# A masked attention layer in 2x2 block products: two PSUM copies taken with a pair's opening products, two weight differences put behind the first sums, adjacency searches put later, the last rows scattered by halves

## The chip, the core and the metric

The kernel runs on one core of one Trainium2 chip. The metric is the device time of one execution in microseconds. Five engines work from queues of their own, each in order: PE (matmul; its weight loads are listed as PEld), DVE (VectorE), ACT (ScalarE), POOL (GpSimd) and SP, which here only issues transfers. POOL issues the indirect transfers (gathers and scatters by row number), ACT a few stores.

## The reference

A graph attention layer over 2708 rows of 1024 float32 features. The adjacency matrix has about four ones in a row.

```
h = relu(layernorm(x))
q, k, v = h @ W_q.T + b_q, h @ W_k.T + b_k, h @ W_v.T + b_v
z = (q @ k.T) / sqrt(1024) * adj;   z = where(z == 0, -10000, z)
out = x + relu(softmax(z, axis=1) @ v)
```

## The kernel before

**Algebra.** `q @ k.T` is `h @ M @ h.T` with `M = W_q.T @ W_k`, computed first (`part_of_m`, L353, 256 recorded matmuls). One neighbour's score is then a dot product of a row of `h @ M` with the neighbour's row of `h`. The weighted sum of the neighbours' rows of h is formed first and multiplied by `W_v` afterwards. Rows are sorted by their number of neighbours, so that a tile of 128 rows takes K gathers.

**Pairs.** The 2708 rows are 21 full tiles and a rest. Two large products (h by M, and weighted sums by `W_v`) are made for pairs of tiles, 10 pairs each, numbered n = 0 to 9 (q pairs) and 10 to 19 (o pairs); tile 0 comes before the q pairs and one sorted tile (`alone`, tile 11) after the o pairs. A pair is a 2x2 block matrix (two tiles by two halves of the features), multiplied by a 2x2 block weight with seven block products in place of eight. The left operands are the blocks `a11`, `a12`, `a22` and the sums `s1` to `s4`; the right operands are the blocks M[i, j] and four differences T[0..3] (`ts_of_m`, L422; one is a [128 x 2048] subtraction on DVE). One block product is four matmuls of 128x512 in the code (`add_block`, L779); the profile records eight for them, since each float32 matmul is recorded twice.

**The order in one pair** (`multiply`, L793). X, Z and Y are PSUM banks of a pool of four. The opening products of the next pair are issued inside the current pair (`opened`, L784): `X += a11 M11` and `Z += s1 T0`. Then, for the pair itself: Y is a copy of X (L799), p5 a copy of Z (L802), both on ACT; `Y += s2 T1`; u2 a copy of Y (L806); `X += a12 M21`, result c11; `Z += s4 M22`, result c12 = Z + u2 (DVE, L844); `Y += s3 T2`, result c22 = Y + p5 (DVE, L841); then the next pair's opening products; `Y += a22 T3`, result c21. So on PE c22 stands between the s3 product and the a22 product of the same bank Y.

**Other work during the pairs.** A function `after(i)` is called between these steps. It transposes the rows of pair n + 1 on PE (`half_turned`, L274), forms s1 to s4 (L529), seeds the banks (L554), and loads the rows of pair n + 2: natural rows (tiles `h_e`, on SP, L562) for n + 2 < FIRST = 5, sorted rows (`qr`, gathered by POOL, L435) from there on. In the first pairs it also runs the rest of the layer norm and of the adjacency reading, from the table `steps_at` (L580): `s16-17` loads x tiles and takes their statistics, `r` takes the root, `a` applies the norm on ACT (L233) and stores h to `h_dram` on POOL, and `eN` (`edges`, L255) loads adjacency tile N (1354 KB, SP, three buffers in turn), sums its rows on ACT (`sized`, L261) and finds its columns with four index searches on DVE (L264) and six small operations.

**The sort.** After all tiles are searched `sort` (L472, called at pair 2, step 3) counts with two matmuls (L493, L495), computes the place of each row (`pos_i`, L507), scatters the table of neighbours to DRAM by place (`put`, L450: 11 indirect stores for the second part, the sorted tiles 11 to 21) and loads it back (`tab`, L461); then come the first gathers of `qr` rows, and the same for the first part.

**Who sets the order.** ACT's order is the program's up to the sort. DVE's order is the program's from pair FIRST on; before that, and for the other engines throughout, a scheduler that works on estimates places the instructions when the kernel is built. All queues are then fixed. From pair FIRST on, a stream of scores and weighted sums (`attention`, L730) is spread over DVE, with gathers on POOL.

**The end.** The lone tile's weighted sum goes through four block products; its result is added to its rows of x (`y_alone`) and written by one indirect store, `scatter` (L616).

Of the kernel before, what the change touches and what calls it, by code (L numbers as in the profile page):

```python
# [10 lines left out]
FT = mybir.dt.float32  # L11
U32 = mybir.dt.uint32
# [3 lines left out]
ALU = mybir.AluOpType  # L16
AX = mybir.AxisListType

P = 128
NB = 512  # L20
# [3 lines left out]
SLOTS = 16  # L24
# [31 lines left out]
def tile_preln_masked_attention(  # L56
# [12 lines left out]
    nc = tc.nc  # L69
    N, D = x.shape  # L70
    DC = D // P
    NH = D // NB
# [17 lines left out]
    psum = ctx.enter_context(tc.tile_pool(name="psum", bufs=4, space=bass.MemoryType.PSUM))  # L90
# [34 lines left out]
    ptab = tab  # L125
# [50 lines left out]
    stat = ph.enter_context(tc.tile_pool(name="stat", bufs=4, side="right"))  # L176
# [242 lines left out]
    def small(name):  # L419
        return half.tile([P, NB], FT, tag="half", name=name, bufs=14)  # L420

    def ts_of_m(*which):  # L422
        flat = M.rearrange("p i j c w -> p i j (c w)")
        t = T.rearrange("p k c w -> p k (c w)")
        for k in which:
            a, b = ((flat[:, 0, 1], flat[:, 0, 0]), (flat[:, 1, 1], t[:, 0]), (flat[:, 1, 1], flat[:, 0, 1]),
                    (flat[:, 1, 0], t[:, 1]))[k]
            nc.vector.tensor_sub(t[:, k], a, b)
# [8 lines left out]
    rows_of = {}  # L437
    FIRST = (EARLY - SINGLE) // 2
# [77 lines left out]
    behind = []  # L516
# [44 lines left out]
            if t > 1:  # L561
                nc.sync.dma_start(row, h_dram[t * P:(t + 1) * P, :])  # L562

    ts_of_m(0, 1, 2, 3)

    nc.vector.tensor_sub(bp_sb[:, NB:], bp_sb[:, NB:], bp_sb[:, :NB])
    natural_rows(0)
# [9 lines left out]
    q = query(hT.pop(0), banks, "e0", first=True, between=('e11 a s16-17', ''), mid=open_first)  # L577
    nc.scalar.dma_start(q_dram[0:P, :], q)

    steps_at = {(0, 0): 'e12 r a e13', (0, 3): 'e14 s18-19 r e15', (1, 0): 'a e16 s20-21 e17', (1, 3): 'e18 r a e19', (2, 0): 'e20 e21'}  # L580
    
    slots, free = [], []

# [16 lines left out]
    def ts_of_wv():  # L600
        with tc.issue_after(placed[0].ins):
            for c in range(4):
                b11, b12 = slots[2 * c][:, :NB], slots[2 * c][:, NB:]
                b22, b21 = slots[2 * c + 1][:, :NB], slots[2 * c + 1][:, NB:]
                nc.vector.tensor_sub(b11, b12, b11)
                nc.vector.tensor_sub(b12, b22, b12)
                nc.vector.tensor_sub(b22, b22, b11)
                nc.vector.tensor_sub(b21, b21, b22)
                for k, r in enumerate((b11, b22, b12, b21)):
                    nc.sync.dma_start(tv_dram[k][:, c, :], r)  # L610
# [5 lines left out]
    outs = []  # L616

    def scatter(y, t, n):
        to = nc.gpsimd.indirect_dma_start(  # L619
            out=out, out_offset=bass.IndirectOffsetOnAxis(ap=ptab.bitcast(U32)[:n, t, SLOTS:SLOTS + 1], axis=0),  # L620
            in_=y[:n], in_offset=None)
        for other in outs:
            tc.declare_no_dep(to.ins, other.ins, reason="rows of a permutation")
        outs.append(to)
# [154 lines left out]
    def add_block(bank, a, b, last=True):  # L779
        for c in range(4):  # L780
            mm = nc.tensor.matmul(bank, a[:, c, :], b[:, c, :], start=False, stop=(c == 3), skip_group_check=True)  # L781
        return mm

    def opened(n):  # L784

        if n not in banks_of:
            return
        X, Z = banks_of[n]
        ops = ops_of[n][0]
        add_block(X, ops["a11"], M[:, 0, 0])  # L790
        products.append(add_block(Z, ops["s1"], T[:, 0]))

    def multiply(n, results, after):  # L793


        X, Z = banks_of.pop(n)
        ops = ops_of.pop(n)[0]
        Y = psum.tile([P, NB], FT, tag="acc", name="psy")
        nc.scalar.copy(Y, X)  # L799
        after(0)  # L800
        p5 = small("p5")
        nc.scalar.copy(p5, Z)  # L802
        after(1)
        products.append(add_block(Y, ops["s2"], T[:, 1]))
        u2 = small("u2")
        nc.scalar.copy(u2, Y)  # L806
        after(2)
        add_block(X, ops["a12"], M[:, 1, 0])
        results[0](X)
        after(3)  # L810
        add_block(Z, ops["s4"], M[:, 1, 1])
        results[2](Z, u2)
        after(4)
        products.append(add_block(Y, ops["s3"], T[:, 2]))
        results[1](Y, p5)
        after(5)
        if n != FIRST - 1:
            opened(n + 1)
        add_block(Y, ops["a22"], T[:, 3])
        results[3](Y)  # L820
        if n == FIRST - 1:

            opened(n + 1)
        after(6)

    lo, hi = slice(0, NB), slice(NB, D)
# [77 lines left out]
    def of_wv(i, j):  # L904

        return wv[j][:, i * 4:(i + 1) * 4, :]
# [4 lines left out]
    alone = order[-1]  # L911
    units = [("q",) + p for p in q_pairs] + [("o",) + p for p in o_pairs]
# [29 lines left out]
    for n, unit in enumerate(units):  # L942
        kind, ta, tb = unit
        now[0] = n
        if n == FIRST:
            ordered.enter_context(tc.manual_schedule(engines={mybir.EngineType.DVE}))
        if FIRST - 1 <= n <= FIRST + 2:

            i, j = ((0, 0), (0, 1), (1, 0), (1, 1))[n - FIRST + 1]
            nc.sync.dma_start(m_dram[i, j], M[:, i, j])  # L950
        share = (20.0 if kind == "q" else 19.0) / 7
        nxt = units[n + 1] if n + 1 < len(units) else None
        results = (q_results if kind == "q" else o_results)(ta, tb)

        def after(i):
            if (n, i) == (2, 3):
                with tc.issue_after(products[-1].ins):
                    placed.append(sort())
                ordered.close()
                ts_of_wv()  # L960
            if n == FIRST - 1 and i == 5:

                chain.append(behind[-1])
                next(stream)
            if n == FIRST - 1 and i == 6:
                chain.append(behind[-1])
            if (n, i) >= (FIRST, 0):
                advance(share)
            if nxt is not None:

                if i == (3 if n == FIRST - 1 else 0):
                    ops_of[n + 1] = blocks(*rows_of[n + 1], nc.gpsimd if n + 1 < FIRST - 1 else None)
                    ops_of[n + 1][1]()
                if i == (4 if n == FIRST - 1 else 2):
                    ops_of[n + 1][2]()
                    rows_of.pop(n + 1)
                    if n == last_q - 1:
                        all_rows()
                if i == 3:
                    banks_of[n + 1] = banks_for(bp_sb)  # L980
                if i == 2 and n + 2 < FIRST:
                    natural_rows(n + 2)
                if i == 4 and n + 2 >= FIRST and n + 2 < len(units) and n + 2 not in rows_of:
                    while units[n + 2][0] == "o" and not done.issuperset(units[n + 2][1:]):
                        advance(1.0)
                    rows_of[n + 2] = load_rows(units[n + 2])
            if (n, i) in steps_at:
                follow(steps_at[n, i])
            if (n, i) == (2, 1):
                searched()  # L990
            if n == last_q - 1 and i == 4:

                nc.sync.dma_start(bp_sb, bv.to_broadcast([P, D]))
                nc.vector.tensor_sub(bp_sb[:, NB:], bp_sb[:, NB:], bp_sb[:, :NB])

            for k, at in enumerate(((0, 0), (0, 1), (0, 3), (0, 4), (0, 5), (0, 6), (1, 2))):
                if (n - last_q, i) == at:
                    place, src = ((M[:, 0, 0], of_wv(0, 0)), (T[:, 0], tv_dram[0]), (T[:, 1], tv_dram[1]),
                                  (M[:, 1, 0], of_wv(1, 0)), (M[:, 1, 1], of_wv(1, 1)), (T[:, 2], tv_dram[2]),
                                  (T[:, 3], tv_dram[3]))[k]  # L1000
                    nc.sync.dma_start(place, src)

        multiply(n, results, after)
# [21 lines left out]
    nc.tensor.matmul(ps_f[:, 0:1], ones, many, start=True, stop=True)  # L1025
    nc.vector.tensor_copy(flag, ps_f[:, 0:1])

    y = work.tile([P, D], FT, tag="q", name="y_alone", bufs=4)
    send(gather(y, x, alone, SLOTS, P))
    tail(NT - 1)  # L1030
    r, = load_rows(("o", alone))
    uT = turned(r, "alone")
    X, Z = banks_for(bp_sb)
# [4 lines left out]
    add_block(Z, uT[:, 4:8, :], M[:, 1, 1])  # L1038
    nc.vector.tensor_add(p1, Z, p1)
    nc.vector.scalar_tensor_tensor(y[:, hi], p1, 0.0, y[:, hi], op0=ALU.max, op1=ALU.add)  # L1040
    add_block(X, uT[:, 4:8, :], M[:, 1, 0])
    nc.vector.scalar_tensor_tensor(y[:, lo], X, 0.0, y[:, lo], op0=ALU.max, op1=ALU.add)
    scatter(y, alone, P)
    ph.close()
    low.close()

# [2 lines left out]
    with tc.If(some > 0):  # L1049
        with tc.tile_pool(name="big", bufs=1, side="right") as big, tc.tile_pool(  # L1050
            name="gen", bufs=1, side="right"
# [19 lines left out]
            with tc.For_i(0, NT) as i:  # L1071
                r0 = nc.snap(smin(i * P, N - P))
                rows = bass.ds(r0, P)
# [20 lines left out]
                for h in range(NH):  # L1094
                    cols = slice(h * NB, (h + 1) * NB)
# [11 lines left out]
                for b0 in range(0, N, NB):  # L1107
                    w = min(NB, N - b0)
# [30 lines left out]
                y = gen.tile([P, D], FT, tag="junk", name="g_y")  # L1139
                for h in range(NH):  # L1140
                    cols = slice(h * NB, (h + 1) * NB)
# [51 lines left out]
```

## Time and profile before

| | us |
|---|---|
| median of 3 runs (694.31 to 695.5) | 695.26 |
| the profiled execution's own time | 695.18 |
| its span, first to last instruction | 693.4 |
| PE busy in the span | 668.1 |
| DVE busy | 526.4 |
| POOL busy | 364.9 |
| ACT busy | 246.8 |
| mean share of the 16 transfer engines, by bytes | 293 GB/s |

The mean granted PE clock is 0.996. A row of a timeline gives the start, the duration, the engine, the line of the code, the operation, output and inputs, the shapes, how many of them are merged, and in brackets the idle time before it with the instruction that ended it. A row of the waits gives the instruction that waited, the one that ended the wait, the total, the number and the longest. The end of a matmul is modelled and reaches into the next one, so an idle time in brackets is some 0.15 us shorter than the distance by starts (a block product that waits for nothing starts 3.43 us after the one before it).

### The profile page before, as it was taken

The page shows a single profiled execution, that of the slowest core. Times are in us where ns is not written, and L with a number is a line of the kernel's source. Part 1 is how long each engine was busy: PE and PEld are TensorE (multiplying, and loading weights), DVE is VectorE, ACT ScalarE, POOL GpSimd, SP SyncE. Part 2 cuts the span into 40 slices and gives each one's busy share as a digit, 9 for nine tenths or more (in the row PEclk, how much of TensorE's full clock was granted, in tenths as well). Part 3 has the DMA queues.
Part 4 walks back from the last instruction along what each step waited for, and adds up shares of the span by engine and source line. Part 5 has one row for each costly group of instructions (what it writes and reads, how often), then busy time and mean ns, then how long its engine had stood idle before and what let it go on. Part 6 is the DMA issues. An engine that isn't in the chain of part 4 may idle for free. (4 is left out here: it accounts for less than half of the span.)

```text
span 693.4 us, 6371 instructions
## 1 busy us (share of the span) xinstructions
PE 668.1 (96%) x1796; PEld 343.3 (50%) x1796; DVE 526.4 (76%) x1053; ACT 246.8 (36%) x374; POOL 364.9 (53%) x309
## 2 busy tenths in 40 slices
PE   6999999989899999999999999999999999999995
PEld 3776777544444444444444444444444444444442
DVE  6999748979999602199988896997887989988301
ACT  0086086366655212323313213233323334323220
POOL 2056163044343656366875453686856887882332
PEclk9999999999999999999999999999999999999998
DMA  9998969989986835789998699999988799895553
GB/s 345 405 383 312 359 217 407 409 336 373 366 288 229 311 102 157 258 282 360 379 369 281 241 414 415 390 332 311 296 245 261 212 283 303 256 267 157 146 145 120
DMA packets 64164, 203.19 MB, mean 293 GB/s; under 512 B 9898, under 2 KB 10250, under 8 KB 62716
## 3 DMA queue, kind: packets, MB, share of 16 engines
q0 software_dynamic: 34448, 109.25, 47.7%
q1 hardware_dynamic: 27660, 86.67, 33.6%
q10 hardware_dynamic: 2016, 6.82, 2.5%
q8 instruction: 16, 0.26, 0.2%
q14 instruction: 24, 0.20, 0.1%
HBM read 166.62 MB, written 49.13 MB: 311 GB/s over the span
## 5 line engine op out<-in xcount | busy, mean ns | idle before, releaser
L433 POOL DMA_INDIRECT g<-h_dram,tab x106 | 132.0, 1246 | 51.5 <-issue 22.1
L781 PE MATMUL psy<-T,s 128*128 128x512 f32 x320 | 144.1, 593 | 1.8 <-ACT psy L799 1.8
L781 PE MATMUL ps<-M,a 128*128 128x512 f32 x320 | 144.1, 592 | 0.0
L665 DVE SCALAR_TENSOR_TENSOR junk<-g,pq 128x1024 uint8<-128x1024 f32 x92 | 112.6, 1224 | 16.9 <-DMA pq<-q_dram,tab 14.7
L360 PE MATMUL ps_m<-wk,wq 128*128 128x512 f32 x256 | 113.9, 607 | 5.6 <-DMA wk<-in_wk_dram 5.6
L718 DVE SCALAR_TENSOR_TENSOR u<-g,coef,u 128x1024 f32<-128x1024 f32 x77 | 98.8, 1283 | 10.9 <-ACT u L710 8.5
L360 PEld LDWEIGHTS ps_m<-wk,wq 128*128 128x128 f32 x256 | 80.2, 315 | 37.2 <-DMA wk<-in_wk_dram 5.6
L781 PEld LDWEIGHTS ps<-M,a 128*128 128x128 f32 x320 | 59.7, 190 | 69.3 <-issue 69.3
L781 PEld LDWEIGHTS psy<-T,s 128*128 128x128 f32 x320 | 59.4, 190 | 69.6 <-issue 69.6
L264 DVE FIND_INDEX8 at<-ones,adj 128x8 uint32<-128x685 f32 (+1 forms) x88 | 75.1, 863 | 0.0
L781 PE MATMUL psy<-T,a 128*128 128x512 f32 x160 | 72.3, 595 | 2.7 <-DVE q L841 2.6
L781 PE MATMUL ps<-M,s 128*128 128x512 f32 x160 | 72.2, 593 | 2.2 <-ACT p L802 2.2
L781 PE MATMUL ps<-T,s 128*128 128x512 f32 x160 | 72.0, 593 | 2.4 <-DVE s L529 2.4
L859 POOL DMA_INDIRECT y<-in_x_dram,tab x21 | 39.3, 1870 | 49.7 <-ACT y L874 19.2
L234 POOL DMA_DIRECT2D h_dram<-x x22 | 12.2, 554 | 89.5 <-ACT x L233 89.5
L261 ACT ACTIVATE sized<-adj 128x2708 uint8<-128x2708 f32 (+1 forms) x22 | 54.2, 2463 | 2.5 <-DMA adj<-in_adj_dram 2.5
L235 POOL TENSOR_TENSOR hsum<-hsum,x 128x1024 f32<-128x1024 f32 (+1 forms) x22 | 52.1, 2369 | 0.3
L781 PEld LDWEIGHTS ps<-T,s 128*128 128x128 f32 x160 | 30.4, 190 | 40.9 <-issue 37.8
L781 PEld LDWEIGHTS psy<-T,a 128*128 128x128 f32 x160 | 30.0, 190 | 41.2 <-issue 34.9
L781 PEld LDWEIGHTS ps<-M,s 128*128 128x128 f32 x160 | 30.1, 190 | 39.3 <-issue 36.1
L710 ACT ACTIVATE u<-g,coef 128x1024 f32<-128x1024 f32 x19 | 21.8, 1149 | 42.7 <-DVE coef L709 35.3
L525 ACT COPY a<-pt 128x512 f32<-128x512 f32 x60 | 33.5, 595 | 8.4 <-PE pt L279 8.4
(193 smaller groups left out, 705.9 us busy)
## 6 DMA issues: line engine op xcount, KB each, us to landing
adj<-in_adj_dram SPq DMA_DIRECT2D x21, 1354.0 KB, 12.3
x<-in_x_dram SPq DMA_DIRECT2D x21, 512.0 KB, 10.2
h_dram<-x POOLq DMA_DIRECT2D x21, 512.0 KB, 6.6
u_dram<-u POOLq DMA_DIRECT2D x14, 512.0 KB, 7.2
or<-u_dram SPq DMA_DIRECT2D x14, 512.0 KB, 8.3
h_e<-h_dram SPq DMA_DIRECT2D x11, 512.0 KB, 10.3
q_late<-q SPq DMA_DIRECT2D x10, 512.0 KB, 7.7
pq<-q_late POOLq DMA_DIRECT2D x10, 512.0 KB, 7.0
```

The costliest lines, as they stand in the source:

```text
L234: nc.gpsimd.dma_start(h_dram[t0:t0 + n, :], xt[:n])
L235: nc.gpsimd.tensor_add(hsum[:n], hsum[:n], xt[:n])
L261: nc.scalar.activation(sized[:n], a[:n, :, :PW], AF.Abs, accum_out=total[:n, t:t + 1])
L264: nc.vector.max_index(at[:n, g, :], ones[:n, 0:8], a[:n, g, :])
L360: nc.tensor.matmul(acc[i], lhs, wk_sb[o][:, cols], start=(o == 0), stop=(o == DC - 1))
L433: return nc.gpsimd.indirect_dma_start(out=dst, out_offset=None, in_=src, in_offset=off, bounds_check=N - 1, oob_is_err=False)
L525: nc.scalar.copy(ops[name], bank)
L665: chained(lambda: nc.vector.scalar_tensor_tensor(junk, g_of[t][s], 1.0, tq[t], op0=ALU.mult, op1=ALU.mult, accum_out=zall[:, t, s:s + 1]))
L710: nc.scalar.activation(u, g_of[t][0], AF.Copy, scale=coef[:, at[t][0]:at[t][0] + 1])
L718: chained(lambda: nc.vector.scalar_tensor_tensor(u, g_of[t][s], coef[:, at[t][s]:at[t][s] + 1], u, op0=ALU.mult, op1=ALU.add))
L781: mm = nc.tensor.matmul(bank, a[:, c, :], b[:, c, :], start=False, stop=(c == 3), skip_group_check=True)
L859: return nc.gpsimd.indirect_dma_start(out=y[:n], out_offset=None, in_=x, in_offset=off, compute_op=ALU.add)
```

## The change

1. The copies of X into Y and of Z into p5 move from `multiply` into `opened`, behind the opening product of each.
2. Of the four differences of M, T[2] and T[3] are formed after pair 0's sums s1 and s3 (`behind[-1]`) and no longer before them.
3. In `steps_at` searches 14 to 19 come one place later; the last place holds three searches and no longer two.
4. The sorted rows of pair 7 are gathered at step 2 of pair 5 and no longer at step 4.
5. The last 128 rows are scattered as two halves of 512 columns, each as soon as it is there. Two small DVE operations (`half_i`) form the row numbers 2r and 2r + 1 from column SLOTS of the lone tile in the reloaded table. They stand near the end of the program text.

```diff
-    ts_of_m(0, 1, 2, 3)
+    ts_of_m(0, 1)
...
+    with tc.issue_after(behind[-1].ins):
+        ts_of_m(2, 3)
+
-    steps_at = {(0, 0): 'e12 r a e13', (0, 3): 'e14 s18-19 r e15', (1, 0): 'a e16 s20-21 e17', (1, 3): 'e18 r a e19', (2, 0): 'e20 e21'}
+    steps_at = {(0,0):"e12 r a e13",(0,3):"s18-19 e14 r",(1,0):"a e15 s20-21 e16",(1,3):"e17 r a e18",(2,0):"e19 e20 e21"}
...
         add_block(X, ops["a11"], M[:, 0, 0])
+        Y = psum.tile([P, NB], FT, tag="acc", name="psy")
+        nc.scalar.copy(Y, X)
         products.append(add_block(Z, ops["s1"], T[:, 0]))
+        p5 = small("p5")
+        nc.scalar.copy(p5, Z)
+        opened_of[n] = Y, p5
...
-        Y = psum.tile([P, NB], FT, tag="acc", name="psy")
-        nc.scalar.copy(Y, X)
+        Y, p5 = opened_of.pop(n)
         after(0)
-        p5 = small("p5")
-        nc.scalar.copy(p5, Z)
         after(1)
...
-                if i == 4 and n + 2 >= FIRST and n + 2 < len(units) and n + 2 not in rows_of:
+                if i == (2 if n == FIRST else 4) and n + 2 >= FIRST and n + 2 < len(units) and n + 2 not in rows_of:
...
+    half_i = stat.tile([P, NH], U32, tag="half_i", name="half_i", bufs=1)
+    for h in range(NH):
+        nc.vector.tensor_scalar(half_i[:, h:h + 1], ptab.bitcast(U32)[:, alone, SLOTS:SLOTS + 1], float(NH), float(h),
+                                op0=ALU.mult, op1=ALU.add)
+
+    def scatter_half(h, cols):
+        to = nc.gpsimd.indirect_dma_start(
+            out=out.rearrange("n (h w) -> (n h) w", h=NH),
+            out_offset=bass.IndirectOffsetOnAxis(ap=half_i[:, h:h + 1], axis=0), in_=y[:, cols], in_offset=None)
...
     nc.vector.scalar_tensor_tensor(y[:, hi], p1, 0.0, y[:, hi], op0=ALU.max, op1=ALU.add)
+    scatter_half(1, hi)
     add_block(X, uT[:, 4:8, :], M[:, 1, 0])
     nc.vector.scalar_tensor_tensor(y[:, lo], X, 0.0, y[:, lo], op0=ALU.max, op1=ALU.add)
-    scatter(y, alone, P)
+    scatter_half(0, lo)
```

More of the change, by code (lines that the diff above doesn't have):

```diff
@@ L782, in add_block @@
         return mm
+    opened_of = {}
     def opened(n):
@@ L1026, in tile_preln_masked_attention @@
     nc.vector.tensor_copy(flag, ps_f[:, 0:1])
+    half_i = stat.tile([P, NH], U32, tag="half_i", name="half_i", bufs=1)
[6 more added lines that the diff above has]
+            out_offset=bass.IndirectOffsetOnAxis(ap=half_i[:, h:h + 1], axis=0), in_=y[:, cols], in_offset=None)
+        for other in outs:
+            tc.declare_no_dep(to.ins, other.ins, reason="rows of a permutation")
+        outs.append(to)
     y = work.tile([P, D], FT, tag="q", name="y_alone", bufs=4)
```

## The prediction

> **What bounds the kernel now.** I read the page first, then PE's waits, then the timelines of PE, DVE and POOL at the places those name. The page:
>
> ```profile
> span 693.4 us, 6371 instructions
> PE 668.1 (96%) x1796; PEld 343.3 (50%) x1796; DVE 526.4 (76%) x1053; ACT 246.8 (36%) x374; POOL 364.9 (53%) x309
> ```
>
> PE is the bound: only what shortens its idle time, its start or the tail behind it counts. Its waits:
>
> ```profile
> PE ps_m L360 <- DMA wk<-in_wk_dram: 5.6, 1, 5.6
> PE psy L781 <- DVE q L841: 2.6, 2, 1.4
> PE ps L781 <- DVE s L529: 2.4, 1, 2.4
> PE ps L781 <- ACT p L802: 2.2, 2, 1.4
> PE psy L781 <- ACT psy L799: 1.8, 2, 0.9
> PE pt L279 <- DMA qr<-h_dram,tab: 1.7, 1, 1.7
> ```
>
> The first is the start, untouched. The rest are where the edits aim. PE's timeline places them:
>
> ```profile
> 145.40 3.67 PE L781 MATMUL ps<-T,s 128*128 128x512 f32 x8 [2.35 <-DVE s L529]
> ...
> 159.98 3.67 PE L781 MATMUL ps<-M,s 128*128 128x512 f32 x8 [1.41 <-ACT p L802]
> ...
> 175.13 3.70 PE L781 MATMUL psy<-T,a 128*128 128x512 f32 x8 [1.18 <-DVE q L841]
> ...
> 180.56 3.67 PE L781 MATMUL psy<-T,s 128*128 128x512 f32 x8 [0.86 <-ACT psy L799]
> ...
> 189.32 3.67 PE L781 MATMUL ps<-M,s 128*128 128x512 f32 x8 [0.78 <-ACT p L802]
> ...
> 208.50 3.67 PE L781 MATMUL psy<-T,s 128*128 128x512 f32 x8 [0.90 <-ACT psy L799]
> ...
> 216.61 0.90 PE L493 MATMUL ps_in<-hot,before 128*128 128x396 f32 x2
> ...
> 253.24 3.60 PE L781 MATMUL ps<-T,s 128*128 128x512 f32 x8
> ...
> 309.97 3.70 PE L781 MATMUL psy<-T,a 128*128 128x512 f32 x8 [1.37 <-DVE q L841]
> ...
> 315.40 1.06 PE L279 MATMUL pt<-ident,qr 128*128 128x128 f32 x8 [1.73 <-DMA qr<-h_dram,tab]
> ```
>
> By starts (3.43 us a product, 0.87 a pair of transposed halves) the seven holes up to 216.61 are 2.51, 1.58, 1.34, 1.03, 0.95, 1.07 and 0.30: 8.78 us, all in pairs 0 to 2. The two at 310 and 315 are 1.53 and 1.99. From 316 to 666 PE has none over 0.3. The rest of the argument needs the sort's table, from DVE's and POOL's timelines:
>
> ```profile
> 223.84 0.18 DVE L507 CAST pos_i<-deg 128x22 uint32<-128x22 f32 x1
> ...
> 239.99 1.28 DVE L529 TENSOR_TENSOR s<-a,pt 128x512 f32<-128x512 f32 x2 [5.62 <-ACT a L525]
> ...
> 245.72 1.06 POOL L461 DMA_DIRECT2D tab<-tab_dram  x1 [5.46 <-DMA tab_dram<-tab,pos_i]
> ...
> 249.43 1.02 POOL L435 DMA_INDIRECT qr<-h_dram,tab  x1 [2.09 <-DMA tab<-tab_dram]
> ...
> 685.87 0.97 POOL L619 DMA_INDIRECT out_dram<-y_alone,tab  x1 [4.03 <-DVE y_alone L1042]
> ```
>
> The places are known to DVE at 224.02, and the reloaded table lands at 249.16 (the trace's semaphore record): 25.14 us later.
>
> **T2 and T3 behind the first sums.** The four subtractions run on DVE from 133.1 to 142.5, 2.2 us each, ahead of s1 at 144.59. Two leave: s1 starts at 140.2, and PE wants it at 142.89. The 2.51 goes, with 2 us to spare once the sum itself is counted. They then stand behind s3, at 141.5 and, behind two statistics whose x tiles land at 144.1 and 145.5, at 146.8 to 149. PE needs T2 at 159 and T3 at 169. Behind them waits the root of x16 and x17, but ACT reaches that only at 150.5. Cost nil.
>
> **The copies.** ACT's p copy of pair 0 ran at 159.27 although Z was ready at 149: it stood behind a 2.46 us `sized` pass, a root, two 1.19 us norm passes and a second `sized` pass. Behind the opening product it runs at about 146.5, and the hole at 159.98 goes; so do 180.56, 189.32 and 208.50, each a copy behind `sized` or norm passes. No copy is added. What queues behind p5 on ACT: transposed blocks and c21, which need later PE work anyway. From pair 6 on, in ACT's new list, p5 passes some `w` and `u` of the score stream; p5 waits for the end of the s1 product, and every `w` or `u` that falls behind it started later than that product's end in the trace of before. Y's copy also needs the c12 sum to have freed its bank, which is 10 us older. Cost nil.
>
> **Searches later.** One search is four index searches of 0.86 and about 1.1 us of small work on DVE, 4.5 us. In the new list pair 0's c12 and c22 stand behind search 14 alone; I get c22 done at 165 (search 14 from 160), PE wants it at 169, so the 1.34 goes. On SP the rows of pairs 3 and 4 now stand ahead of adjacency tile 18, and one of them waits for x18's store to `h_dram`. That store I put at 181.4 (188.26 before), so tile 18 is issued at 181.7, 8 us later than before, tiles 19 to 21 earlier (182.3, 187, 196 against 188.8, 189.5, 194). With the 8 to 12 us that these loads took before, search 21 ends at 207.7, against 211.7.
>
> **The sort.** Without holes PE reaches the old place of its count at 216.61 − 8.78 = 207.83. In the new list eight matmuls of 0.86 us go ahead of it (three of s4, two of the next a11, three of s3): 214.7. DVE has `hot` at 207.7 + 3.4 for the counting + c12, s1, s3 and hot 2.5 = 213.6. So PE sets it: places known at 214.7 + 7.4 (as before) = 222.1, table landed at 222.1 + 25.1 = 247.2.
>
> **The two `half_i` operations.** Though written at the program's end, the scheduler has put them on DVE right behind the differences of W_v and ahead of pair 4's s1, s3, s2, s4 and pair 3's c12 and c22, with a wait for the table's load. Before, that s1 ran at 239.99 in an idle stretch. Now DVE stands from about 232 to 247.2. Then two operations of 0.2 and s1 of 0.6 with its semaphores: PE's s1 product can start at 248.4. PE without holes would be there at 253.24 − 8.78 = 244.5. So 3.9 us of the 8.8 come back as one stall: the first stage yields 253.24 − 248.4 = **4.8 us**. s2 to c22 are five more operations of 0.65 to 0.7, done at 251.5, before PE ends the product at 251.8.
>
> **Pair 7's rows.** The two gathers, 1.3 us each on POOL, go ahead of a q gather, a g gather, a store of u and two M gathers. Issued about 299 in the old time, they land at 307, PE wants them at 313.4: **2.0 us**. The works they pass move about 2.6 to 3.8 us; the M gathers then land about 313.9 and 315.2, and DVE reads them at 314.75 and 316.47. The hole at 309.97 stays: c22 stands between scores that start when q_dram's last rows are back (291.62), and that start is tied to PE. Later c22 sums were 1.8 to 6 us early; DVE waits for PE at 346 and 352 (0.7 and 1.5 us), where it takes up the 2 us.
>
> **The end.** The trace gives 3.46 us from issue to landing of the last 512 KB (685.87 to 689.33), and GpSimd's own closing drain, a record that the views leave out, lasts from 686.38 to 692.55, 3.2 us beyond the landing. [...] By the row it is nothing, as the second half is issued at the same moment and the drain outlasts the landing. Bounds: 0.9 gained, 0.5 lost (a drain over two stores); I take 0, the row's.
>
> **Sum.** 4.8 + 2.0 + 0 = 6.8. The profiled execution's 695.18 becomes 688.4; the median of the runs is 0.08 above it: **688.5**.
>
> **Rivals.**
> *The block on DVE does not bite* (the wait met earlier than I read it): 8.8 + 2.0 = 10.8, 684.5. For it: DVE is idle at the place. Against: the new list shows the wait, on the load that the first qr gather waits for too. 0.08.
> *The sort slips by 2 to 5 us:* every microsecond that search 21 is late beyond 208.8 goes to the table and, by DVE's block, to PE. The transfer engines are near full here (373 and 366 GB/s between 156 and 191). 690.5 to 693.5. 0.14.
> *Slower: the same wait, decisive.* Tiles 18 to 21 behind the row that waits for x18's store; if the places are known only after 224.02 + 4.8 + 0.1 = 228.9, the table lands after 254 and the whole first gain is gone; at 231 or later the pair 7 gain too, 696 to 699. That needs the last loads 9 us behind my times. 0.10.
> *The edits do not do what they say* (copies still late on ACT behind other passes, c22 still late): 692 to 696. 0.06.
> The forecast: 0.62.
>
> **How the numbers follow.** A measurement of this kernel tells about 0.2%, 1.4 us. Faster than 693.9: 0.62 + 0.08 + 0.13 + 0.02 = 0.85; same 0.05; slower 0.10. The range 686.0 to 692.8 leaves out the unblocked case, the slower one and a little of the fourth; its low end is the tail's 0.9 and the 1.5 at 310 together, its high end a sort 4 us late.
>
> **What would show it.** Right: no PE wait on p L800, psy L797 or on s of pair 0; one new PE wait of about 4 us on s (L529) near 245; in DVE an idle stretch of some 15 us ended by the table's load, at L1037; pos_i near 222; no wait on qr. Wrong: no such idle time (then 684 to 685), or pos_i after 226; or a last L619 row whose tail to the span's end is not about 7.5 us.

## The result and the profile after

| | time, us (median; lowest to highest) | ratio to the kernel before, 95% interval |
|---|---|---|
| before | 695.26 (692.66 to 697.58, 11 runs) | |
| changed | 689.81 (688.28 to 695.0, 11 runs) | 0.9932 [0.9906, 0.9957] |
| changed, again, in a later set (g2) | 691.6 (690.57 to 694.58, 6 runs; before there 693.74) | 0.9959 [0.9944, 0.9975] |

The changed kernel is faster, by 5.5 us in one set and 2.1 in the other; 6.8 was forecast for the profiled execution, and 688.5 for the median. Its profiled execution took 690.05 us, its span is 688.3. The page:

```profile
span 688.3 us, 6376 instructions
PE 667.5 (97%) x1796; PEld 343.5 (50%) x1796; DVE 527.3 (77%) x1055; ACT 248.5 (36%) x374; POOL 367.6 (53%) x310
```

PE's waits, complete (total, number, longest). Gone are p, the copies' psy and qr; new are hot and a tiny u, and s now stands for pair 4:

```profile
PE ps_m L360 <- DMA wq<-in_wq_dram: 5.4, 1, 5.4
PE psy L784 <- DVE q L848: 2.6, 1, 2.6
PE ps_in L493 <- DVE hot L489: 1.9, 1, 1.9
PE ps L784 <- DVE s L529: 1.8, 1, 1.8
PE psy L784 <- ACT u L813: 0.3, 1, 0.3
```

PE's timeline at those places, and at 141.30, where the hole of 2.51 us was:

```profile
137.87 3.60 PE L784 MATMUL ps<-M,a 128*128 128x512 f32 x8
141.30 3.60 PE L784 MATMUL ps<-T,s 128*128 128x512 f32 x8
...
157.21 3.70 PE L784 MATMUL psy<-T,s 128*128 128x512 f32 x8 [0.27 <-ACT u L813]
...
215.28 0.90 PE L493 MATMUL ps_in<-hot,before 128*128 128x396 f32 x2 [1.94 <-DVE hot L489]
...
247.06 3.67 PE L784 MATMUL ps<-T,s 128*128 128x512 f32 x8 [1.84 <-DVE s L529]
...
298.89 3.60 PE L784 MATMUL ps<-T,s 128*128 128x512 f32 x8
305.08 5.40 PE L784 MATMUL psy<-T,a 128*128 128x512 f32 x8 [2.59 <-DVE q L848]
310.32 1.04 PE L279 MATMUL pt<-ident,qr 128*128 128x128 f32 x8
311.19 3.60 PE L784 MATMUL psy<-T,s 128*128 128x512 f32 x8
```

By starts the holes are 0.43, 2.10, 2.01 and 2.76 us. The a22 product at 305.08 lasts 5.40 us and no longer 3.6. DVE's side of it:

```profile
212.69 2.45 DVE L489 TENSOR_TENSOR hot<-deg,down 128x198 f32<-128x198 f32 x2
...
221.72 0.18 DVE L507 CAST pos_i<-deg 128x22 uint32<-128x22 f32 x1
...
246.10 0.22 DVE L1037 TENSOR_SCALAR half_i<-tab 128x1 uint32<-128x1 uint32 x2 [14.58 <-DMA tab<-tab_dram]
246.23 1.27 DVE L529 TENSOR_TENSOR s<-a,pt 128x512 f32<-128x512 f32 x2
...
286.74 1.23 DVE L668 SCALAR_TENSOR_TENSOR junk<-g,pq 128x1024 uint8<-128x1024 f32 x1 [15.88 <-DMA pq<-q_dram,tab]
...
304.34 0.69 DVE L848 TENSOR_TENSOR q<-psy,p 128x512 f32<-128x512 f32 x1
```

The ledger, from starts. PE's first a11 product began 1.58 us earlier than before (137.87 against 139.45), in a stretch that the change does not touch; in the fourteen traces of this case that start lies between 137.87 and 139.50, so this is the spread of one profile. From there to pair 4's s1 product 113.79 us became 109.19: **4.60 gained**. From there to pair 6's s2 product (311.19) 63.06 became 64.13: **1.07 lost**. From there to the last row of PE's products nothing changed (361.52 in both). The tail, from the last issue to the end of the span, is 7.52 us before and 7.60 after. 1.58 + 4.60 − 1.07 − 0.08 = 5.03, within rounding of the difference of the spans, 5.05.

The middle term is where the forecast of 2.0 went wrong. The windows of the changed kernel (busy PE, granted clock, share of the DMA engines, GB/s) show the first half of why:

```profile
core 0: us, PE busy (x), PEclk, DMA share, GB/s
...
300.00:305.00 5.00, 2.49 (x6) 1.00 0.96 338
305.00:310.00 5.00, 4.92 (x8) 0.66 1.03 415
310.00:315.00 5.00, 5.00 (x22) 1.00 1.01 344
```

Behind the hole PE ran at half clock: the trace's clock record has one stretch at 0.5, from 305.97, 3.41 us long. The eight matmuls took 1.8 us longer for it. The second half is the hole itself, 2.76 us where it had been 1.53.

### The profile page after: what moved, and what is told of

The parts are those of the page before. It is cut to its first block, busy times and chain, and to the rows that moved or that the text cites. A ratio compares the mean times of both kernels' runs of the same rounds, so it can differ in the third digit from the quotient of the medians.

```text
span 688.3 us, 6376 instructions
## 1 busy us (share of the span) xinstructions
PE 667.5 (97%) x1796; PEld 343.5 (50%) x1796; DVE 527.3 (77%) x1055; ACT 248.5 (36%) x374; POOL 367.6 (53%) x310
## 3 DMA queue, kind: packets, MB, share of 16 engines
q10 hardware_dynamic: 2016, 6.82, 2.6%
## 4 chain that ended last, share of the span: by engine, by line
PE 84%; DMA 4%; issue 4%; DVE 4%; ACT 2%; POOL 2%; SPq 0%; POOLq 0%; ACTq 0%; DVEq 0%
PE ps L784 34%; PE psy L784 26%; PE ps_m L360 16%; PE pt L279 5%; PE ps L313 2%; POOL tab_dram L454 2%; ACT sized L261 1%; DMA g<-in_wv_dram 1%; DVE junk L668 1%; DVE u L721 1%; DMA wq<-in_wq_dram 1%; DMA pq<-q_dram,tab 1%; DMA tab_dram<-tab,pos_i 1%; PE ps_v L380 0%; DMA tab<-tab_dram 0%
## 5 line engine op out<-in xcount | busy, mean ns | idle before, releaser
L784 PE MATMUL psy<-T,a 128*128 128x512 f32 x160 | 73.9, 606 | 2.7 <-DVE q L848 2.6
L866 POOL DMA_INDIRECT y<-in_x_dram,tab x21 | 36.4, 1734 | 50.6 <-ACT y L881 20.2
L235 POOL TENSOR_TENSOR hsum<-hsum,x 128x1024 f32<-128x1024 f32 (+1 forms) x22 | 53.6, 2438 | 0.4
```

The source lines that it names most:

```text
L235: nc.gpsimd.tensor_add(hsum[:n], hsum[:n], xt[:n])
L866: return nc.gpsimd.indirect_dma_start(out=y[:n], out_offset=None, in_=x, in_offset=off, compute_op=ALU.add)
```

## The experiments

All times are medians; each ratio is to the kernel before, measured in the same set of runs. Where two kernels of different sets are compared, it is by these ratios. "From the first a11 product" means that the difference of the starts above is taken out, which compares two traces more finely than their spans do.

**e1_halves_late.** half_i behind DVE's last scores.

```diff
-    for h in range(NH):
-        nc.vector.tensor_scalar(half_i[:, h:h + 1], ...
+    with tc.issue_after(chain[-1].ins):
+        for h in range(NH):
+            nc.vector.tensor_scalar(half_i[:, h:h + 1], ...
```

> The two half_i operations stand behind DVE's last scores; all else is the changed kernel. Theory (the block on DVE costs PE time): no idle stretch of DVE ends at half_i; pair 4's s1 runs in DVE's idle time near 240, and PE's hole of 2.02 us ahead of pair 4's s1 product (247.06 in the changed kernel's trace) goes. That gain can be kept only as far as the next hole lets it: PE then reaches pair 5's c22 hole (305.08) 2.0 us earlier, and c22 stands there among scores that hang on the table's landing (246.07) and on the last q store, which moves with PE. If that store comes back 2 us earlier, the time falls by 2.0, to about 687.8. Rival (c22's place is tied to POOL's gathers, which start at the table's landing and do not move): the hole at 305 grows from 2.75 to about 4.7 us and the time stays within 0.7 of 689.8, or is longer, as a longer hole lets the granted clock fall to half for 3.41 us in more of the runs (1.7 us each).

Measured: 689.5 us, 0.9938 [0.9915, 0.9961]. PE's timeline at the count and at c22:

```profile
215.97 0.91 PE L493 MATMUL ps_in<-hot,before 128*128 128x396 f32 x2 [1.93 <-DVE hot L489]
...
217.40 1.92 PE L784 MATMUL psy<-T,s 128*128 128x512 f32 x2
...
304.77 5.40 PE L784 MATMUL psy<-T,a 128*128 128x512 f32 x8 [1.99 <-DVE q L848]
310.01 1.04 PE L279 MATMUL pt<-ident,qr 128*128 128x128 f32 x8
```

The hole at pair 4's s1 product is gone, exactly its 2.01 us; DVE's block cost that. The hole on c22 did not grow, it is 2.15. But a stretch at half clock now also followed the count's hole of 2.09 us at 215.97 (the two matmuls at 217.40 take 1.92 us and not 1.02), and took 1.7 us back. In its six runs the mean granted clock is 0.990 to 0.994, never more. Gain from the first a11 product: 1.1 us; in the medians nothing that can be told from the changed kernel.

**e2_c22_early.** Three steps of the score stream behind pair 5's c12 and c22.

```diff
-                advance(share)
+                advance(share - 3.9 * ((n, i) == (FIRST, 3)) + 3.9 * ((n, i) == (FIRST, 5)))
```

> The changed kernel with three steps of the score stream (about 3.7 us of DVE) put behind pair 5's c12 and c22 sums and no longer ahead of them. Theory: PE's hole of 2.75 us at pair 5's a22 product goes, and with it the stretch of half clock of 3.41 us that follows it in the changed kernel's trace (305.97 to 309.38; 1.7 us lost). The profile shows no wait on q L848 and no stretch below full clock before the end; the time falls by 2.7 in a run without the half clock and by 4.4 in one with it: 685.4 to 687.1, median near 686.3, and the spread of the runs shrinks. Rival (the work put behind c22 is late for something else, the sums u that free gather buffers or pair 6's s sums): a new hole of 1 to 3 us behind 316 and a time of 688 to 690.

Measured: 691.78 us, 0.9974 [0.9958, 0.9991]: not 686. The hole and its half clock went, and 3.8 us were in hand at pair 6's s2 product (307.93). They were lost at one place 54 us further on, as e2's PE timeline shows:

```profile
303.62 3.60 PE L784 MATMUL psy<-T,a 128*128 128x512 f32 x8
307.06 1.04 PE L279 MATMUL pt<-ident,qr 128*128 128x128 f32 x8
...
361.93 1.94 PE L279 MATMUL pt<-ident,qr 128*128 128x128 f32 x8 [3.14 <-DMA qr<-h_dram,tab]
```

Those are pair 9's rows. Their first gather is issued by GpSimd at 350.46 behind a row of g and q gathers and lands at 361.80. A new stretch at half clock came with it. The rival's kind was right, its place was not: rows, not sums.

**e3_c22_late.** One more score ahead of that c22.

```diff
-                advance(share)
+                advance(share - -1.3 * ((n, i) == (FIRST, 4)) + -1.3 * ((n, i) == (FIRST, 5)))
```

> The changed kernel with one more score (1.25 us of DVE) ahead of pair 5's c22 sum. It prices the hole. Theory (a hole of over about 2.6 us is followed by 3.41 us at half clock, whatever its cause): the hole grows to 4.0 us, nearly every run has the half-clock stretch, so that the time is 1.25 longer in all runs and 1.7 longer in those that were spared before: median 691.5 to 693. Rival (the half clock in the one trace was chance and not the hole's): median 691.0, with the half clock in no more runs than before.

Measured: 693.12 us, 0.9994 [0.9978, 1.001]. The hole was 4.86 us, 1.26 for the score and 0.84 because pair 4's last q rows came back later in that run. All twelve runs have a mean clock of 0.992 to 0.995; in the first set of the changed kernel four of eleven had 0.997. The theory's count holds; the median lies just above its 691.5 to 693.

What the two experiments share is how the hole on c22 is made. Pair 5's scores start when pair 4's last q rows are back: SP stores them (L841), GpSimd gathers them into pq (L435). Take the time from the issue of that store to the landing of the first pq, and the hole on c22:

| kernel | store issued to pq landed, us | hole, us | difference |
|---|---|---|---|
| before | 280.89 to 291.60: 10.71 | 1.54 | 9.17 |
| e1 | 275.08 to 286.41: 11.33 | 2.15 | 9.18 |
| changed | 274.78 to 286.71: 11.93 | 2.76 | 9.17 |
| f1 (below) | 276.77 to 288.75: 11.98 | 2.80 | 9.18 |
| f2 (below) | 275.83 to 289.24: 13.41 | 4.23 | 9.18 |

The hole is that transfer less 9.2 us, in kernels whose PE reaches the place up to 6 us apart. The other traces in which the scores stand as in the changed kernel agree: f3 (11.44 and 2.27), g1 (12.69 and 3.50) and g2 (12.09 and 2.96) differ by 9.1 to 9.2, and in g4, with 9.22, there is no hole. So the start of the scores does move with PE, and the hole is only as long as a store and a gather of 512 KB take. The store alone took 5.86 us before and 6.82 in the changed kernel, 5.7 to 7.9 over the five traces of the table. In the changed kernel it is issued 6.1 us earlier while the g gathers ahead of it on GpSimd (269.40 to 275.89) are only 2.4 us earlier, so that they run into each other; that this is what lengthened it was not tried by itself. One trace speaks for it (in g4 the store is issued 3.6 us after the last of these gathers and takes 4.3 us), one against it (in e1 three of them are still to come and it takes 5.7).

**e4_both.** e1, and four steps behind c12 and c22 (5.2 for 3.9).

> half_i behind DVE's last scores, and four score steps put behind pair 5's c12 and c22. Theory: both holes go, the gains add: 2.0 and 2.7 to 4.4, so 683.4 to 685.1. Rival: the scores that hang on the table are the next limit, and the 2.0 of half_i come back as waits of PE on c12, c22 or s sums behind 316: 685.5 to 687.

Measured: 689.21 us, 0.9954 [0.9932, 0.9977]. From the first a11 product it led the changed kernel by 6.6 us at pair 6's s2 product and by 2.0 at the end: 0.70 us went to pair 8's rows at 331.42 and 3.54 to pair 9's at 360.78. Both holes went, as the theory had it, but the time is longer than theory or rival gave: the waits that came in their place were for rows.

**f1_pair7_back.** Pair 7's rows at step 4 of pair 5, as before.

```diff
-                if i == (2 if n == FIRST else 4) and n + 2 >= FIRST ...
+                if i == 4 and n + 2 >= FIRST ...
```

> The changed kernel, with pair 7's rows gathered at step 4 of pair 5 as before. It asks what this edit is worth. The prediction's step said 2.0 us. Theory (the hole on c22 ahead of it had grown and swallowed it): GpSimd issues the first row gather at about 302.4 where the changed kernel issues it at 294.2, it lands at about 310.4, and PE wants it at 308.5 where no half-clock stretch follows the c22 hole and at 310.3 where one does. So a wait on qr of 1.9 at most comes back, and of nearly nothing in runs with the half clock: 0 to 1.9 longer than the changed kernel, median near 1. Rival (the step was right in full): 2.0 longer in every run, whatever the clock.

Measured: 692.04 us, 0.9976 [0.996, 0.9991]. In the trace no wait on qr came back: the hole on c22 (2.80) and its half clock had PE late enough, and from pair 4 to the end the trace runs level with the changed kernel's (the 0.7 us that it is behind there were lost at the count, which the edit does not touch). So in such an execution the edit is worth nothing. By the ratios it is worth 1.2 us beside 0.9959, where the intervals overlap, or 3.1 beside 0.9932, where they do not; what it is on average stays open.

**f2_whole_row.** The last 128 rows scattered whole, no half_i.

```diff
-    scatter_half(1, hi)
...
-    scatter_half(0, lo)
+    scatter(y, alone, P)
```

> The changed kernel with the last 128 rows scattered whole, as before; there is then no half_i and no block on DVE. Beside the kernel that only puts half_i late, it prices the halves at the end by themselves. Theory (the end is set by GpSimd's closing drain, which outlasts the landing): from the issue of the last scatter to the end of the span 7.5 us, as in both traces; the time equals that of the kernel with half_i late, a ratio to the kernel before of 0.994. Rival (the shorter landing counts): 0.7 slower than that one.

Measured: 690.61 us, 0.9946 [0.9929, 0.9963], beside 0.9938 [0.9915, 0.9961] for e1. GpSimd's last rows, of f2 and then of the changed kernel:

```profile
683.28 0.97 POOL L622 DMA_INDIRECT out_dram<-y_alone,tab  x1 [4.15 <-DVE y_alone L1049]
```

```profile
678.12 0.98 POOL L1041 DMA_INDIRECT out_dram<-y_alone,half_i  x1 [1.53 <-DVE y_alone L1060]
680.75 0.96 POOL L1041 DMA_INDIRECT out_dram<-y_alone,half_i  x1 [1.65 <-DVE y_alone L1063]
```

From the last issue the half lands in 2.74 us and the whole row in 3.62, yet to the end of the span it is 7.60 us with the halves and 7.52 with the whole row: the shorter landing does not bring the end forward.

**f3_copies_back.** The copies of X and Z back in `multiply`.

```diff
-        Y = psum.tile([P, NB], FT, tag="acc", name="psy")
-        nc.scalar.copy(Y, X)
         products.append(add_block(Z, ops["s1"], T[:, 0]))
-        p5 = small("p5")
-        nc.scalar.copy(p5, Z)
...
+        Y = psum.tile([P, NB], FT, tag="acc", name="psy")
+        nc.scalar.copy(Y, X)
+        after(0)
+        p5 = small("p5")
+        nc.scalar.copy(p5, Z)
```

> The changed kernel with the copies of X and Z back in the pair's own program, as before. The holes behind them summed to 4.6 us before. Theory (what is gained ahead of the sort's count is kept only until DVE's hot and then the table): the holes at about 158, 180, 189 and 208 come back, 4.6 us, but PE's wait of 2.1 us for hot at 215 is gone, so the count and with it the table's landing and pair 4's s1 product come 2.1 to 2.5 later, not 4.6: 2.1 to 2.5 longer than the changed kernel, median near 691.5. Rival (the parts add up): 4.6 longer, 694.

Measured: 694.82 us, 1.0013 [0.9995, 1.0031]. PE's waits on the copies are back:

```profile
PE ps L784 <- ACT p L807: 3.7, 2, 3.0
PE psy L784 <- DVE q L846: 3.6, 2, 2.1
PE psy L784 <- ACT psy L804: 1.8, 2, 0.9
```

The theory fell in both steps. The count came no later than in the changed kernel (77.3 us behind the first a11 product, against 77.4), because the scheduler put it ten recorded matmuls, 4.3 us, further ahead in PE's list; yet PE was 3.9 us later at pair 4's s1 product, by its own holes: 3.12, 1.03, 0.94 and 1.07 on the copies and 1.68 on c22, less the 2.1 and the 2.0 that it no longer waited for hot and for s, and 0.4 for u. At the end 3.4 us remain, and the medians say 4 to 6. Undone alone, the copies take back more than pair 7's rows or the searches do; T2 and T3 were not put back alone. Each such edit also moves what the scheduler places after it, so the parts need not add up.

**f4_rows_early.** e4, and the rows of pairs 8 and 9 at step 2.

```diff
-                if i == (2 if n == FIRST else 4) and n + 2 >= FIRST ...
+                if i == (2 if FIRST <= n <= last_q - 2 else 4) and n + 2 >= FIRST ...
```

> The kernel with half_i late and four score steps behind pair 5's c12 and c22, in which PE then waited for pair 9's rows (3.5 us, at 360.8) and pair 8's (0.7, at 331.4); here the rows of pairs 8 and 9 are gathered at step 2 of the pair two ahead, as pair 7's are. Theory (the gain of the first two edits had turned into the wait for these gathers): both waits go, no other hole over 0.5 us stands between 216 and 660, and the time falls by 4.2 to a little under 685 (span 683). Rival (the gathers of g and q that they overtake are late in their turn): a wait of DVE on g or pq that holds c12 or c22 sums back, and PE waits of 2 us or more between 320 and 420: 687 to 689.

Measured: 685.93 us, 0.9884 [0.9868, 0.99], faster than both kernels. The waits for rows are gone:

```profile
PE ps_m L360 <- DMA wq<-in_wq_dram: 5.5, 1, 5.5
PE ps_in L493 <- DVE hot L489: 1.9, 1, 1.9
PE psy L784 <- DVE q L848: 0.9, 1, 0.9
PE psy L784 <- ACT u L813: 0.6, 1, 0.6
```

That is where the gains of e2 and e4 had gone: here a lead of 5.4 us over the changed kernel at pair 6's s2 product is still 5.0 at the end. The 0.9 is new, on pair 4's c22 at 270.17.

**g1_searches_back.** `steps_at` as before, all else as changed.

```diff
-    steps_at = {(0,0):"e12 r a e13",(0,3):"s18-19 e14 r",(1,0):"a e15 s20-21 e16",(1,3):"e17 r a e18",(2,0):"e19 e20 e21"}
+    steps_at = {(0, 0): 'e12 r a e13', (0, 3): 'e14 s18-19 r e15', (1, 0): 'a e16 s20-21 e17', (1, 3): 'e18 r a e19', (2, 0): 'e20 e21'}
```

> The changed kernel with the searches in their old places. Theory (the last search carries the table, the table carries half_i and DVE): pair 1's c22 hole of 1.3 us comes back but is swallowed by the wait for hot at 215; search 21 ends near 211, 2 later than in the changed kernel (209.2); hot, the count, the places and the table follow, and the hole ahead of pair 4's s1 product grows from 2.0 to about 4.0: 2.0 longer, and up to 1.7 more where so long a hole is followed by a stretch at half clock: a median 2 to 3.5 above the changed kernel's. Rival (the searches do not carry the end): no more than the 1.3 of the hole.

Measured: 692.96 us, 0.9982 [0.9969, 0.9994], 1.4 above the changed kernel's 691.6 in the same set. In the trace it is 2.4 from the first a11 product beside the first profile of the changed kernel, but 1.7 of that is one more stretch at half clock; g2's profile, with three stretches to g1's two, is 1.2 longer than g1's. Of its way there only one row was as I had thought, search 21 later (1.4 us by the start of PE's first a11 product, at 212.21). DVE's hot:

```profile
214.92 0.64 DVE L489 TENSOR_TENSOR hot<-deg,down 128x198 f32<-128x198 f32 x2
```

It took 0.64 and not 2.45, and that paid for the late search: the table landed 108.22 us behind the first a11 product, 108.20 in the changed kernel. What was lost was PE's own: the hole on pair 1's c22 was 4.19, as PE without the other holes gets there sooner, and half clock followed it (1.72):

```profile
173.46 4.88 PE L784 MATMUL psy<-T,a 128*128 128x512 f32 x7 [4.03 <-DVE q L848]
```

**g2_changed_again.** The changed kernel as it is.

> The changed kernel itself, so that its runs stand beside those of the others on one chip. Expected: a ratio to the kernel before of 0.993, and times that go with the granted clock, as each stretch of 3.41 us at half clock is 0.0025 of the mean clock and 1.7 us of time: runs at 0.997 near 688.5, at 0.995 near 690, at 0.992 near 692. Rival (the spread has other causes): no order between clock and time.

Measured: 691.6 us, 0.9959 [0.9944, 0.9975], a smaller gain than 0.993, and not a run at 0.997. Clock and time go together, though not strictly: 690.57 and 691.34 at 0.995, 691.87 at 0.994, 691.1 and 692.67 at 0.992, 694.58 at 0.988; in the first set 688.3 to 689.8 at 0.997 and 693.3 and 695.0 at 0.990, but also 688.97 at 0.995 and 688.7 at 0.993. Its profiled execution, the one at 0.988, has half clock behind the hole at pair 4's s1 product (2.16) and 6.83 us of it behind c22's (2.96). From the first a11 product it takes 554.08 us, where the first profile of the same kernel takes 550.48 with one stretch, and the kernel before 553.94 with none: two stretches more are 3.4 of the 3.6 us between the two profiles of one kernel, and as much as the change had gained in the first.

**g3_s_on_dve.** f4, with pair 3's s2 and s4 on DVE.

```diff
-                    ops_of[n + 1] = blocks(*rows_of[n + 1], nc.gpsimd if n + 1 < FIRST - 1 else None)
+                    ops_of[n + 1] = blocks(*rows_of[n + 1], nc.gpsimd if n + 1 < FIRST - 2 else None)
```

> The kernel of f4_rows_early with pair 3's s2 and s4 formed on DVE and no longer on GpSimd. It asks why the two hot operations took 2.45 us where they took 0.64 in the kernel before. Theory (they ran beside GpSimd's two tensor sums and had to share a way to SBUF with them): with GpSimd quiet they take 0.32 each; hot ends 0.5 earlier, as DVE now does 1.4 us of sums itself; PE's wait of 2.1 us at the count falls to about 1.1 (PE arrives 0.43 later there); the time falls by 0.5 at most. Rival (they are slow by their own operands or for another reason): 1.2 each as before, hot ends 1.4 later, the wait grows and the time rises by 1 or more.

Measured: 684.6 us (683.64 to 687.25, 5 runs), 0.9872 [0.9851, 0.9893], the lowest median; beside f4's the intervals overlap, and from the first a11 product its trace is 1.05 us ahead. DVE of f4 and, below it, GpSimd of f4:

```profile
213.57 2.45 DVE L489 TENSOR_TENSOR hot<-deg,down 128x198 f32<-128x198 f32 x2
```

```profile
213.19 1.27 POOL L529 TENSOR_TENSOR s<-s,a 128x512 f32<-128x512 f32 x1 [3.88 <-DMA g<-in_wv_dram]
214.54 1.26 POOL L529 TENSOR_TENSOR s<-a,s 128x512 f32<-128x512 f32 x1
```

DVE of g3:

```profile
214.17 0.36 DVE L489 TENSOR_TENSOR hot<-deg,down 128x198 f32<-128x198 f32 x1
214.45 0.68 DVE L529 TENSOR_TENSOR s<-a,s 128x512 f32<-128x512 f32 x1
215.05 0.35 DVE L489 TENSOR_TENSOR hot<-deg,down 128x198 f32<-128x198 f32 x1
```

With GpSimd quiet each hot takes 0.35 us, near the theory's 0.32. In f4 the two end 0.22 us behind the end of GpSimd's first and second sum. The way to SBUF that the two share in the theory is not shown by itself; the traces show the times. The wait for hot fell from 2.11 to 0.62 us.

**g4_hot_first.** f4, with the sort written one step earlier.

```diff
-            if (n, i) == (2, 3):
+            if (n, i) == (2, 2):
```

> The kernel of f4_rows_early with the sort written one step earlier in pair 2; DVE's list then has hot ahead of pair 3's s1 and s3. Theory: hot takes 0.64 and ends near 212.5 (in the changed kernel's time), PE does not wait at the count, places and table come 1.5 to 2 earlier, and the time falls by 1.5 to 2 to about 684. Rival (s1 and s3 now stand behind sums of the sort that wait for the count): PE waits 1 us or more for s1 of pair 3 near 221, or for c12 and c22 further on, and the time stays within 0.7 of 685.9 or rises.

Measured: 691.41 us, 0.9952 [0.9936, 0.9968], worse than f4. The step itself did as the theory said (hot 0.63 us, no wait at the count), and then, in g4's PE timeline:

```profile
242.40 3.68 PE L279 MATMUL pt<-ident,h_e 128*128 128x128 f32 x16 [6.98 <-DMA h_e<-h_dram]
```

The sort now precedes the loads of pair 4's rows in the program. In SP's list they moved behind the last four adjacency tiles, sixteen loads of W_v, sixteen stores of its differences and two of q, and are issued at 235.86, where in f4 they were issued ahead of all these, by 180.9. PE ran at half clock from 237.90 on, for the length of three such stretches: the seven matmuls at 245.86 take 4.30 us, where seven in e1 at 322.06 take 3.17. The rival named another wait; neither theory saw this one.

## Why the prediction was right, and where it was not

**The number came near in part by luck.** Of the 5.05 us between the two spans, 1.58 lie ahead of the first product that the change touches. What the two traces show of the change is 3.5 us, about half of the 6.8 forecast: the first stage held, pair 7's 2.0 did not come. In the medians it is 5.5 us in one set and 2.1 in the other.

**T2 and T3: right.** The s1 product starts 3.43 us behind a11; the 2.51 is gone.

**Copies: right.** All the holes on copies are gone, and no p or psy copy is waited for; "cost nil" fails only by the 0.43 us on u at 157.21. f3 bears the size out roughly (the four holes were 4.6 us; 3.4 at the end in its trace, 4 to 6 in the medians).

**Searches: right for the hole, for a partly wrong reason.** Pair 1's c22 hole went. Search 21 ended at 209.16 and not 207.7. The loads did not set that: tile 18 was issued at 180.06, earlier than the 181.7 forecast, and DVE had no idle time from 189.67 to the end of search 21. But one small operation of a search, which takes 0.18 us elsewhere, stood 2.11 us beside a GpSimd sum; DVE's row, then GpSimd's:

```profile
195.11 2.11 DVE L267 SCALAR_TENSOR_TENSOR cand<-at,cand 128x32 f32<-128x32 uint32 x1
```

```profile
194.79 2.36 POOL L235 TENSOR_TENSOR hsum<-hsum,x 20x1024 f32<-20x1024 f32 x1
```

That search 21 also carries the table is not shown: in g1 it ended later and the table did not, but hot was 1.8 us shorter there, and g1 does not separate the two.

**"So PE sets it": wrong.** DVE set the count, and PE waited 2.10 us for hot. The failed term is "c12, s1, s3 and hot 2.5", in which hot stood with the 0.64 of the trace before; moved beside GpSimd's s2 and s4 it took 2.45, and the term 4.2. Hot of before, then GpSimd's sums of the changed kernel, beside its hot at 212.69:

```profile
215.82 0.64 DVE L489 TENSOR_TENSOR hot<-deg,down 128x198 f32<-128x198 f32 x2
```

```profile
212.31 1.27 POOL L529 TENSOR_TENSOR s<-s,a 128x512 f32<-128x512 f32 x1 [3.88 <-issue]
213.65 1.26 POOL L529 TENSOR_TENSOR s<-a,s 128x512 f32<-128x512 f32 x1
```

Other terms were off too and in part cancel: the counting took 1.7 and not 3.4, search 21 ended 1.5 later than forecast, and PE came 1.5 earlier (at 213.2 and not 214.7, as its first a11 product was 1.58 earlier). With hot at its old length PE would have waited some 0.3 us (an estimate: 2.1 less 1.8); g3, in which hot is short, has 0.62. Measured from the first a11 product, the table was still on time: 108.2 us against the forecast's 107.75, as 25.1 us from places to table became 24.2.

**half_i: right.** DVE stood idle 14.58 us until the table, and pair 4's s1 product came 109.19 us behind the first a11 product, 108.95 forecast. The stall itself was 2.01 and not 3.9, because PE had already waited for hot. e1 and f2, without that block on DVE, have no hole there. The first stage gave 4.60 for a forecast of 4.8.

**Pair 7's rows: wrong.** The 1.99 us wait on qr did go, but f1 shows that behind the longer c22 hole it goes without the edit too; the step that failed is "The hole at 309.97 stays". It grew by 1.2, the store and the gather of pair 4's last q rows taking 11.93 us and not 10.71, and half clock took 1.8 behind it: 2.0 − 1.2 − 1.8 is the 1.07 lost, within rounding. I had asked when the scores start and not how long the transfer before them takes among gathers that had not moved with it.

**The end: right**, at 0 (f2). No run shows the 0.9 gained that the prediction set as a bound and took into the low end of its range: from the last issue the half lands in 2.74 us and the whole row in 3.62, and the end of the span comes 7.60 and 7.52 us after that issue (f2 the latter), so the landing is not what ends the span here.

**The clock was in no step.** This is the gap in the working. Some of PE's holes were followed by half clock and some were not:

| hole, us | where | clock behind it |
|---|---|---|
| 2.01, 2.10 | changed: pair 4's s1, the count | full |
| 2.51 | before: pair 0's s1 | full |
| 3.54 | e4: pair 9's rows | full |
| 2.09, 2.15 | e1: the count, c22 | half |
| 2.16, 2.96 | g2: pair 4's s1, c22 | half |
| 2.76 | changed: c22 | half |
| 2.80 | f1: c22 | half |
| 4.19 | g1: pair 1's c22 | half |
| 7.15 | g4: pair 4's rows | half |

Over the fourteen traces 9 of the 18 holes of 2.05 to 3.41 us were followed by half clock. The 2.6 us of e3's theory is no limit, as 2.09 us was followed by it and 3.54 was not. The length of a hole alone does not tell, and what else decides is not shown.

A single stretch is 3.41 us long at a granted clock of 0.5: 1.8 us lost in the changed kernel, 1.72 in g1. If a hole of this size is followed by half clock as often as not (an estimate, from the 9 of 18), the changed kernel with its 2.10 and 2.76 loses about one stretch in an execution, and the kernel before with its 2.51 half of one. Shrinking holes to just over 2 us leaves that chance open, and by g2's runs it is a good part of the spread of one kernel.

The mean granted clock counts these stretches only roughly, as PE also stands at half clock in the idle tail behind its last product, for 3.2 to 6.5 us of the span in these traces (3.5 in the changed kernel, 5.7 in the kernel before), a difference as large as one stretch. By an estimate from these figures, a mean of 0.996 or more has no stretch, one of 0.994 or less at least one, and 0.995 can be either.

## What to carry to other kernels

Removing a wait on the bounding engine shows the next one behind it, which may be late rows or one transfer: follow each later consumer up to where it stops being early, and ask of each transfer how long it takes among the traffic it will then meet. When an operation moves in time, price it by what runs beside it at the new place, not by its old duration. Read the granted clock behind each hole of PE; in these traces half clock followed 9 of the 18 holes of 2.05 to 3.41 us and cost 1.7 to 1.8 us a stretch beyond the hole, and behind one of 2.96 us (g2) it lasted two stretches, 6.83 us.

## What the runs showed of the hardware that was not expected

- Half clock behind some of PE's holes, in stretches of 3.41 us: the shortest hole that was followed by it was 2.09 us (e1), and one of 3.54 us (e4) was not. At 0.5 eight matmuls of 128x512 took 5.40 us, at full clock 3.60.
- Some DVE operations took longer beside GpSimd's sums. The two hot operations, whose operands are in SBUF, take 0.35 us each in g3 and took 1.11 and 1.42 in the changed kernel beside two GpSimd sums, each ending 0.22 us behind the GpSimd sum. Over the fourteen traces the 18 hot operations that began beside a GpSimd sum took 1.10 to 1.42 us, the other 10 about 0.36; 15 c22 sums, which have one operand in PSUM, began beside one and took 0.67 to 0.69, as elsewhere. The trace of before had it already: at 186.27 an operation of a search (L266) that takes 0.18 us elsewhere took 2.44 beside GpSimd's sum of hsum.
- A 512 KB store and the gather that reads it took 10.7 to 13.4 us from one trace of the table to the next (the store alone 5.7 to 7.9), and all of the difference reached PE.
